# A drain at the end of each of TensorE's steps, and two buffers moved out of their pools, in a graph network layer

## The chip, the core and the metric

The kernel runs on one core of a Trainium2 chip. The core has TensorE (PE in the profile; its weight loads are PEld), VectorE (DVE), ScalarE (ACT), GpSimd (POOL) and SyncE (SP). Each works through its own queue in order, and they wait for one another by semaphores. The metric is the time of one execution on the device in microseconds (us). Of the kernel before there are 17 runs.

## The reference

One layer of message passing on a graph, with a residual and a layer norm. There are 12,500 nodes of 64 features and 212,500 edges of 32 features, sorted by their destination. All is float32.

```python
msg_in = concatenate([nodes[row], nodes[col], edge_features])        # 64 + 64 + 32
messages = relu(msg_in @ mW1 + mb1) @ mW2 + mb2                      # 128, then 64
aggregated = segment_sum(messages, col, num_segments=nodes.shape[0])
upd_in = concatenate([nodes, aggregated])
x = layernorm(nodes + relu(upd_in @ uW1 + ub1) @ uW2 + ub2)
```

Here `row` is an edge's source and `col` its destination.

## The kernel before, in words

Edges are worked in 554 groups (`G`) of 384 (`GE`), each three tiles of 128. Since edges are sorted, the destinations of one group lie in a window of 32 nodes (`W`) from a start that DVE reads into a register. The second product of the message MLP is folded into the update, so that only the hidden layer (128 wide) is summed for each node.

A group `g` goes through three parts on TensorE, each in a bank of its own of one of two PSUM buffers (`own.ps[g % 2]`):

- `turn` (L360): three transposes of the gathered source rows and of the one-hot of destinations beside them. ACT copies the result into `own.st` (L372), where edge features already lie, and keeps the counts.
- `hidden` (L392): three products with `wm`, which holds the source's weights, the window's 32 rows (the destinations' share of the first layer) and the edge features' weights. ACT applies the relu (L401).
- `sums` (L419, L422): one small transpose of the counts and three products that add the hidden rows to the window's nodes. DVE adds them to `agg` (L431) and the counts to a row of `xc` (L432).

A *step* `k` (`step`, L502) puts these parts together on TensorE's queue: turn of group `k`, hidden of `k - 2`, sums of `k - 4`. Once in four steps, for a block of four groups (`SB`), one more product follows at the step's end: `windows` (L310), the columns of destinations `xw` with `w1b`. DVE copies its four parts into the `wm` tiles (L315). All waits of a step are laid on its first instruction, and all but its last instruction raise no semaphore. What follows a step waits for that last instruction, `did[-1]`: ACT's copy and relu, DVE's adds and copies, and the load of edge features for a later block (SP, L284). In the last ten groups (`SHORT`) the parts are steps of their own.

Gathers run on POOL's queue, one indirect DMA for each tile of 128 rows (L145), 16 groups ahead (`AHEAD`) in a ring of 20 (`RING`). The gather of group `g` waits for ACT's copy of group `g - 20`. In 52 groups the middle tile is not gathered: DVE (L349) or ACT (L350) copies its 128 columns one by one from `xc`, the transposed nodes on the chip, a few after each step (`copies_of`). These are the copied columns.

DVE's queue has, in the order of the program: the one-hot of group `k + 1` (L324), the adds of step `k`, with the window step the four `wm` copies, the column copies, and once in four steps the copies of destinations' columns into `xw` (L303). TensorE's step `k + 2` uses the same PSUM buffer as step `k`, and so waits for ACT's copy and relu and for DVE's adds of step `k`.

Twenty-five times, when a run of 512 nodes has all of its edges, `update` puts its own products into TensorE's queue behind a step (L449, L450, in the next step L462). They write a PSUM buffer from a pool, and ACT (L452) and DVE (L464) wait for them by TensorE's semaphore.

`own` holds buffers allocated outside the pools, for which the framework tracks nothing: their order is what `after` says (L109). Before the change, `xw` is a pool of two tiles and `w1b` a tile of the pool of constants; the product L310, which reads both, is then always the last of its step.

Of the kernel before, what the change touches and what calls it, by code (L numbers as in the profile page):

```python
# [10 lines left out]
F32 = mybir.dt.float32  # L11
# [11 lines left out]
D = 64  # L23
DE = 32
H = 128
# [3 lines left out]
W = 32  # L29
TG = 3  # L30
GE = TG * P
G = (E + GE - 1) // GE
SB = 4
# [3 lines left out]
NW = 2 * SB  # L37
# [3 lines left out]
CH = 512  # L41
# [3 lines left out]
SHORT = 10  # L45
# [36 lines left out]
class Own:  # L82
# [4 lines left out]
    def __init__(self, nc, ctx):  # L87
        def on(name, *shape, of=nc.sbuf_tensor):
            return ctx.enter_context(of(name, list(shape), F32)).ap()

        self.s = [on(f"own_s{i}", P, TG, D + W) for i in range(RING)]
        self.st = [on(f"own_st{i}", P, SB * GE) for i in range(BLOCKS)]
        self.wm = [on(f"own_wm{i}", P, H) for i in range(NW)]
        self.h = [on(f"own_h{i}", P, TG, H) for i in range(NH)]

        self.f = {way: [on(f"own_f{len(way)}_{i}", P, P) for i in range(2)]
                  for way in (BY_DVE, BY_ACT)}
        self.ident = on("own_ident", P, P)
        self.counts = on("own_counts", D + W, G)

        self.ps = [on(f"own_ps{i}", P, 3, 512, of=nc.psum_tensor) for i in range(2)]
# [3 lines left out]
def ordered(ctx: ExitStack, tc: tile.TileContext, a, own, ok):  # L105
# [3 lines left out]
    nc = tc.nc  # L109
    x, out = a["x"], a["out"]  # L110
    const = ctx.enter_context(tc.tile_pool(name="const", bufs=1))
    xwp = ctx.enter_context(tc.tile_pool(name="xw", bufs=2))
    iop = ctx.enter_context(tc.tile_pool(name="iota_ps", bufs=1, space=PSUM))
    ups = ctx.enter_context(tc.tile_pool(name="upd_ps", bufs=1, space=PSUM))
    early = ctx.enter_context(ExitStack())
# [9 lines left out]
    nc.sync.dma_start(src_sb[:, :first], a["src"][:, :first])  # L125

    loads, places_by, copy_by, relu_by, sums_by, wm_by, turn_by = ({} for _ in range(7))
    efs_by, hidden_by, columns_by = {}, {}, {}
    held = {ET.DVE: [], ET.Activation: []}

    def after(first, *others):

        tc.declare_no_dep(first.ins, group="quiet", reason="waits for the last of a step")
        for i in others:
            tc.add_manual_dep(
                first.ins, i.ins.name,
                mybir.DependencyInfo(mybir.DependencyClass.Sync, mybir.DependencyReason.DATA),
                reason="the kernel's own rings",
            )
        return first  # L140
# [36 lines left out]
    xc = const.tile([D + 2, NP], F32, name="xc")  # L177
# [4 lines left out]
    nc.sync.dma_start(dlc_i, a["dst_cols"])  # L182
    nc.sync.dma_start(xc[D : D + 1, :].rearrange("o (p n) -> o p n", p=P), zero)
    nc.sync.dma_start(xc[D + 1 :, :].rearrange("o (p n) -> o p n", p=P), ones[:, : NP // P])
    w1b = const.tile([D + 2, H], F32, name="w1b")
    nc.vector.memset(w1b[D : D + 1, :], 0.0)
    nc.scalar.dma_start(w1b[:D, :], a["mW1"][D : 2 * D, :])
    nc.scalar.dma_start(w1b[D + 1 :, :], a["mb1"][None, :])
# [102 lines left out]
    def places(b):  # L291

        g, n = b * SB, min(SB, G - b * SB)
        if n <= 0:
            return
        _, v = nc.values_load_multi_w_load_instructions(
            start_i[0:1, g : g + n], engines=[ET.DVE], min_val=0, max_val=N - 1,
            skip_runtime_bounds_check_because="they were clamped to the nodes on the chip",
        )
        xw = xwp.tile([D + 2, SB, W], F32, name="xw")  # L300
        for i in range(n):
            starts[g + i] = v[i]
            nc.vector.tensor_copy(xw[:, i, :], xc[:, bass.ds(v[i], W)])  # L303
        xws[b] = xw, n

    def windows(b, wp, own_bank=True):


        xw, n = xws.pop(b)
        did = nc.tensor.matmul(wp[: n * W, :], xw[:, :n, :], w1b, start=True, stop=True)  # L310

        def copies():
            for i in range(n):
                g = b * SB + i
                c = nc.vector.tensor_copy(wm[g % NW][D : D + W, :], wp[i * W : (i + 1) * W, :])  # L315
                after(c, *([did] if own_bank else []), *([hidden_by[g - NW]] if g >= NW else []))
                wm_by[g] = c

        return did, copies

    def onehot(g):
        if g >= G:
            return
        places_by[g] = nc.vector.tensor_tensor(  # L324
            own.s[g % RING][:, :, D:], iota.unsqueeze(1).to_broadcast([P, TG, W]),
            dlc[:, g * TG : (g + 1) * TG].unsqueeze(2).to_broadcast([P, TG, W]), ALU.is_equal,
        )
        after(places_by[g], *([sums_by[g - RING]] if g >= RING else []))
# [161 lines left out]
    def step_update(g):  # L490

        nonlocal now
        if not now and waiting and waiting[0][0] <= g:
            steps = waiting.pop(0)[1]
            now = [steps[0](), *steps[1:]]
        elif now:
            got = now[1](now[0])
            now = [got, *now[2:]] if len(now) > 2 else []
# [3 lines left out]
    def step(*work):  # L502


        parts, used = [], []
        for part, g in work:
            ps, old = own.ps[g % 2], users[part][g % 2]
            parts.append((part, g, *part(g, ps)))
            used += old
        did = [i for p in parts for i in p[2]]  # L510
        after(did[0], *used, *(i for p in parts for i in p[3]))
        copies = None
        for part, g, *_ in parts:
            if part is sums:
                for b in [b for b in xws if (b - 1) * SB <= g][:1]:
                    last, copies = windows(b, own.ps[g % 2][:, 2, (TIMES + 1) * W :][:, :H])
                    did.append(last)
        for i in did[:-1]:
            tc.no_tile_sem_insts.add(i.ins.name)
            tc.add_to_no_dep_group("quiet", i.ins)  # L520
        for part, g, _, _, follow in parts:
            if part is sums:
                step_update(g)
            users[part][g % 2] = follow(did[-1])
            if part is sums and copies:
                copies()
                users[part][g % 2] += [wm_by[b * SB + i] for i in range(min(SB, G - b * SB))]

    inputs(0)
    inputs(1)  # L530
    places(0)
    windows(0, ups.tile([H, CH], F32, name="u_ps")[:, :H], False)[1]()
    onehot(0)
    made = summed = 0

    for k in range(G):
        if k < BITS:
            bit(k)
        if k % SB == 2:
            inputs(k // SB + 2)  # L540
        if k % SB == 1:
            places(k // SB + 1)
        onehot(k + 1)
        if k < G - SHORT:
            step((turn, k), *([(hidden, k - 2)] if k > 1 else []),
                 *([(sums, k - 4)] if k > 3 else []))
            made, summed = max(0, k - 1), max(0, k - 3)
        else:

            step((turn, k))  # L550
            for _ in range(2):
                if summed < made:
                    step((sums, summed))
                    summed += 1
            for _ in range(2):
                if made <= k:
                    step((hidden, made))
                    made += 1
        if k + AHEAD < G:
            gather(k + AHEAD)  # L560
        copies_of(k)
# [285 lines left out]
@with_exitstack  # L847
def gnn_layer(ctx: ExitStack, nc, a):
    own = Own(nc, ctx)
    tc = ctx.enter_context(tile.TileContext(nc))  # L850
    flag = ctx.enter_context(tc.tile_pool(name="flag", bufs=1))
    ok = flag.tile([1, 1], I32, name="ok")
    with tc.manual_schedule():
        ordered(tc, a, own, ok)
    good = nc.values_load(ok[0:1, 0:1], min_val=0, max_val=1,
                          skip_runtime_bounds_check_because="a comparison's result")
    with tc.If(good == 0):
        with tc.manual_schedule():
            unordered(tc, a)
# [36 lines left out]
```

## Time and profile before

| | us |
|---|---|
| median of 17 runs | 2686.57 |
| lowest, highest | 2680.12, 2695.09 |
| the profiled execution | 2690.23 |
| its span, first to last instruction | 2688.4 |

| engine | busy us | share of the span |
|---|---|---|
| TensorE, products | 1677.7 | 62% |
| TensorE, weight loads | 1448.7 | 54% |
| GpSimd (gathers) | 1519.0 | 57% |
| VectorE | 1060.7 | 39% |
| ScalarE | 827.1 | 31% |

The mean granted clock of TensorE is 0.79 of full speed. A group of the profile has its line, engine, operation and tiles (what it writes, then what it reads), the count, busy time and mean duration, and then the engine's idle time just before these instructions, with what ended most of it. "Issue" as a releaser is time in which the profile shows nothing waited for; "remote" is a releaser that it couldn't name. A product in float32 is recorded as two products and two weight loads. Ends of products are modelled.

### The profile page before, as it was taken

How to read it: one execution, taken by the hardware profiler on the slowest of the kernel's cores; microseconds unless marked ns; L12 is line 12 of the kernel's file. 1: busy time of each engine (PE TensorE's matmuls, PEld its weight loads, DVE VectorE, ACT ScalarE, POOL GpSimd, SP SyncE). 2: the span in 40 equal slices, each digit the busy share in tenths (PEclk: the TensorE clock that was granted, in tenths of full speed). 3: DMA queues.
4: the chain of work that ended last, by engine and by line, in shares of the span. 5: the costliest groups of instructions: out<-in, count | busy, mean ns of one | idle time of the engine just before them, and what ended most of it. 6: DMA issues, size and time to landing. Idle time of an engine off the chain costs nothing.

```text
span 2688.4 us, 45023 instructions
## 1 busy us (share of the span) xinstructions
PE 1677.7 (62%) x9545; PEld 1448.7 (54%) x9545; DVE 1060.7 (39%) x7163; ACT 827.1 (31%) x4455; POOL 1519.0 (57%) x1616
## 2 busy tenths in 40 slices
PE   0466666666666765665656665757566666666577
PEld 0355555555555655555645555656555555555565
DVE  4124344344343443443434434444344343443423
ACT  0123333333333333333323333333333333332322
POOL 7565555555555555555555555555555555555550
PEclk9677777778777777878778778788777777887878
DMA  3211111111111111111111111111111111111110
GB/s 76 62 40 37 35 32 36 33 34 34 33 37 32 35 35 34 32 36 33 34 32 34 37 29 37 32 35 34 35 32 36 30 36 31 35 37 32 35 33 14
DMA packets 71877, 95.29 MB, mean 35 GB/s; under 512 B 32632, under 2 KB 40075, under 8 KB 71595
## 3 DMA queue, kind: packets, MB, share of 16 engines
q0 software_dynamic: 51488, 52.80, 10.3%
q1 hardware_dynamic: 19193, 39.06, 5.3%
q8 instruction: 81, 1.33, 0.2%
q14 instruction: 201, 1.65, 0.2%
q10 hardware_dynamic: 914, 0.46, 0.1%
HBM read 88.90 MB, written 3.20 MB: 34 GB/s over the span
## 4 chain that ended last, share of the span: by engine, by line
PE 48%; issue 18%; another core or an unknown queue 18%; ACT 10%; ACTq 3%; DVE 3%; DMA 0%; DVEq 0%
PE own_ps L422 18%; PE own_ps L392 15%; PE own_ps L360 9%; ACT own_h L401 3%; ACT own_st L372 3%; ACT own_f L350 3%; ACTq L343 2%; PE own_ps L419 2%; PE u_ps L462 1%; PE u_ps L449 1%; ACTq L350 1%; PE own_ps L310 1%; PE u_ps L450 1%; DVE agg L431 1%
## 5 line engine op out<-in xcount | busy, mean ns | idle before, releaser
L145 POOL DMA_INDIRECT own_s<-in_x,src_sb x1609 | 1518.2, 944 | 1091.4 <-ACT own_st L372 670.4
L360 PE MATMUL own_ps<-own_ident,own_s 128*96 128x128 f32 x1661 | 364.9, 342 | 915.7 <-issue 736.9
L372 ACT ACTIVATE own_st<-own_ps 96x384 f32<-96x384 f32 (+2 forms) x606 | 286.2, 472 | 1703.3 <-PE own_ps L422 1043.6
L360 PEld LDWEIGHTS own_ps<-own_ident,own_s 128*96 128x96 f32 x1661 | 225.6, 159 | 992.6 <-issue 794.2
L422 PE MATMUL own_ps<-own_s,own_h 128*128 128x128 f32 x3322 | 641.6, 341 | 0.1
L392 PE MATMUL own_ps<-own_wm,own_st 128*128 128x128 f32 (+1 forms) x3322 | 628.2, 337 | 1.4 <-DVE own_wm L315 1.4
L431 DVE TENSOR_TENSOR agg<-own_ps,agg 128x32 f32 x554 | 105.3, 190 | 1218.0 <-ACT own_h L401 1119.0
L392 PEld LDWEIGHTS own_ps<-own_wm,own_st 128*128 128x128 f32 (+1 forms) x3322 | 569.5, 250 | 16.3 <-issue 11.3
L422 PEld LDWEIGHTS own_ps<-own_s,own_h 128*128 128x128 f32 x3322 | 520.1, 234 | 27.1
L349 DVE COPY own_f<-xc 64x1 f32 x3968 | 428.4, 144 | 213.9 <-issue 209.1
L350 ACT ACTIVATE own_f<-xc 64x1 f32 x2688 | 304.4, 193 | 8.7 <-issue 5.9
L401 ACT ACTIVATE own_h<-own_ps 128x384 f32<-128x384 f32 x553 | 263.3, 476 | 18.8 <-PE own_ps L392 13.5
L315 DVE COPY own_wm<-own_ps 32x128 f32<-32x128 f32 x550 | 157.0, 285 | 5.9 <-issue 0.3
L324 DVE TENSOR_TENSOR own_s<-iota,dlc 128x96 f32<-128x96 f32 x554 | 135.9, 246 | 12.3 <-issue 7.1
L432 DVE TENSOR_TENSOR xc<-own_ps,xc 1x32 f32 x554 | 101.1, 183 | 27.8 <-PE u_ps L450 5.9
L419 PE MATMUL own_ps<-own_ident,own_counts 32*1 32x32 f32 x554 | 106.9, 193 | 3.8 <-ACT own_st L372 1.9
L372 ACT ACTIVATION_READ_ACCUMULATOR own_st<-own_ps 96x1 f32 (+1 forms) x554 | 106.4, 192 | 0.6
L303 DVE COPY xw<-xc 66x32 f32 x554 | 80.0, 210 | 50.2 <-issue 49.3
L419 PEld LDWEIGHTS own_ps<-own_ident,own_counts 32*1 32x1 f32 x554 | 41.1, 74 | 93.7 <-issue 47.5
L310 PE MATMUL own_ps<-w1b,xw 66*128 66x128 f32 (+1 forms) x276 | 57.1, 290 | 0.0
L462 PE MATMUL u_ps<-u,u 128*128 128x64 f32 (+1 forms) x196 | 48.7, 398 | 9.8 <-ACT u L452 9.8
L462 PEld LDWEIGHTS u_ps<-u,u 128*128 128x128 f32 (+1 forms) x196 | 47.2, 324 | 11.3 <-ACT u L452 11.1
(63 smaller groups left out, 337.1 us busy)
## 6 DMA issues: line engine op xcount, KB each, us to landing
own_st<-in_efT SPq DMA_DIRECT2D x138, 192.0 KB
own_s<-in_x,src_sb POOLq DMA_INDIRECT x1609
xin<-in_x SPq DMA_DIRECT2D x24, 128.0 KB
out<-o SPq DMA_DIRECT2D x24, 128.0 KB
xc<-in_xT SPq DMA_DIRECT2D x12, 179.2 KB
dlc_i<-in_dst_cols SPq DMA_DIRECT2D x1, 831.0 KB
xc<-in_xT SPq DMA_DIRECT2D x4, 179.5 KB
src_sb<-in_src SPq DMA_DIRECT2D x13, 50.5 KB
```

The source lines that it names most:

```text
L145: nc.gpsimd.indirect_dma_start(out=s[:p, j, :D], out_offset=None, in_=x[:, :], in_offset=bass.IndirectOffsetOnAxis(ap=src_sb[:p, g * TG + ...
L315: c = nc.vector.tensor_copy(wm[g % NW][D : D + W, :], wp[i * W : (i + 1) * W, :])
L324: places_by[g] = nc.vector.tensor_tensor(own.s[g % RING][:, :, D:], iota.unsqueeze(1).to_broadcast([P, TG, W]), dlc[:, g * TG : (g + 1) * ...
L349: c = (nc.vector.tensor_copy(*column) if engine == ET.DVE else nc.scalar.activation(*column, AF.Copy))
L350: else nc.scalar.activation(*column, AF.Copy))
L360: nc.tensor.transpose(xt[:, j * P : j * P + p], s[:p, j, :], ident[:p, :p])
L372: nc.scalar.activation(t[to, c : c + m], xt[to, :m], AF.Copy, **({"accum_out": counts[to, g : g + 1]} if to.stop > D else {})), step)
L392: did.append(nc.tensor.matmul(pre[:p, j, :], edges, weights, start=i == 0, stop=i == len(parts) - 1))
L401: relu_by[g] = [nc.scalar.activation(h, pre, AF.Relu)]
L419: did = [nc.tensor.transpose(line, counts[lo:, g : g + 1], ident[lo : D + W, lo : D + W])]
L422: did.append(nc.tensor.matmul(sg, h[:p, j, :], s[:p, j, D:].unsqueeze(1).to_broadcast([p, TIMES, W]), start=j == 0, stop=j == len(sizes) - 1))
L431: after(nc.vector.tensor_tensor(agg[:, at], sg[:, 0, :], agg[:, at], ALU.add), step),
```

## The change

At the end of each step, behind its last product and ahead of any update's products, TensorE gets a `drain`: an instruction of its sequencer that waits until the engine has finished. It comes in every step whose first part has a group under 544 (`G - SHORT`). The drain becomes `did[-1]`; so all products of a step, the window product too, raise no semaphore, and what followed the last product now waits for the drain. That drain's semaphore belongs to TensorE's sequencer, another one than the engine's own. The products of the updates keep the engine's own.

So that L310 can be one of the silent instructions, its operands `xw` (two buffers) and `w1b` are moved to `own`. The order that the pool kept is written out: DVE's copies into `xw` for block `b` wait for the step that read the buffer for block `b - 2` (`wide_by`).

```diff
@@ class Own
+        self.xw = [on(f"own_xw{i}", D + 2, SB, W) for i in range(2)]
+        self.w1b = on("own_w1b", D + 2, H)
@@ ordered
-    xwp = ctx.enter_context(tc.tile_pool(name="xw", bufs=2))
...
-    w1b = const.tile([D + 2, H], F32, name="w1b")
+    w1b = own.w1b
@@ places
-        xw = xwp.tile([D + 2, SB, W], F32, name="xw")
+        xw = own.xw[b % 2]
         for i in range(n):
             starts[g + i] = v[i]
-            nc.vector.tensor_copy(xw[:, i, :], xc[:, bass.ds(v[i], W)])
+            after(nc.vector.tensor_copy(xw[:, i, :], xc[:, bass.ds(v[i], W)]),
+                  *([wide_by[b - 2]] if b > 1 else []))
@@ windows
-        def copies():
+        def copies(step):
+            wide_by[b] = step
             for i in range(n):
                 g = b * SB + i
                 c = nc.vector.tensor_copy(wm[g % NW][D : D + W, :], wp[i * W : (i + 1) * W, :])
-                after(c, *([did] if own_bank else []), *([hidden_by[g - NW]] if g >= NW else []))
+                after(c, step, *([hidden_by[g - NW]] if g >= NW else []))
@@ step
+        if work[0][1] < G - SHORT:
+            did.append(nc.tensor.drain())
         for i in did[:-1]:
             tc.no_tile_sem_insts.add(i.ins.name)
...
             if part is sums and copies:
-                copies()
+                copies(did[-1])
@@ before the loop
-    windows(0, ups.tile([H, CH], F32, name="u_ps")[:, :H], False)[1]()
+    did, copies = windows(0, ups.tile([H, CH], F32, name="u_ps")[:, :H])
+    copies(did)
```

More of the change, by code (lines that the diff above doesn't have):

```diff
@@ L127, in ordered @@
     loads, places_by, copy_by, relu_by, sums_by, wm_by, turn_by = ({} for _ in range(7))
-    efs_by, hidden_by, columns_by = {}, {}, {}
+    efs_by, hidden_by, columns_by, wide_by = {}, {}, {}, {}
     held = {ET.DVE: [], ET.Activation: []}
@@ L299, in places, with windows @@
         )
-        xw = xwp.tile([D + 2, SB, W], F32, name="xw")
+        xw = own.xw[b % 2]
         for i in range(n):
             starts[g + i] = v[i]
-            nc.vector.tensor_copy(xw[:, i, :], xc[:, bass.ds(v[i], W)])
+            after(nc.vector.tensor_copy(xw[:, i, :], xc[:, bass.ds(v[i], W)]),
+                  *([wide_by[b - 2]] if b > 1 else []))
         xws[b] = xw, n
-    def windows(b, wp, own_bank=True):
+    def windows(b, wp):
         xw, n = xws.pop(b)
         did = nc.tensor.matmul(wp[: n * W, :], xw[:, :n, :], w1b, start=True, stop=True)
-        def copies():
+        def copies(step):
+            wide_by[b] = step
             for i in range(n):
```

## The prediction, made before the changed kernel ran

> **What bounds the kernel now.** I read the page's totals first, then the waits, then the timeline of a few steps, then the end of the kernel. No engine is full, and GpSimd (POOL) with its gathers is the one with most left to do one after the other:
>
> ```profile
> PE 1677.7 (62%) x9545; PEld 1448.7 (54%) x9545; DVE 1060.7 (39%) x7163; ACT 827.1 (31%) x4455; POOL 1519.0 (57%) x1616
> ...
> PEclk9677777778777777878778778788777777887878
> ...
> L145 POOL DMA_INDIRECT own_s<-in_x,src_sb x1609 | 1518.2, 944 | 1091.4 <-ACT own_st L372 670.4
> ```
>
> The waits say who holds whom; the columns are engine and line, what released it, us in total, times, longest:
>
> ```profile
> DVE agg L431 <- ACT own_h L401: 1119.0, 289, 45.6
> ACT own_st L372 <- PE own_ps L422: 1043.6, 248, 6.9
> PEld own_ps L360 <- issue: 794.2, 273, 10.2
> ...
> POOL own_s L145 <- ACT own_st L372: 670.4, 271, 9.9
> ACT own_st L372 <- remote: 494.0, 80, 18.7
> ```
>
> POOL waits 670 us for ScalarE's copy of a step (the ring of gathered tiles is full), DVE waits for ACT, ACT waits for TensorE, and TensorE waits in turn. A circle of waits has a slow link somewhere. The timeline shows it (start, duration, engine, line; idle time before in brackets):
>
> ```profile
> 1480.13 0.39 PE L310 MATMUL own_ps<-w1b,xw 66*128 66x128 f32 x2
> ...
> 1481.92 0.94 PE L422 MATMUL own_ps<-own_s,own_h 128*128 128x128 f32 x6
> 1482.04 0.94 POOL L145 DMA_INDIRECT own_s<-in_x,src_sb  x1 [0.30 <-issue]
> 1484.55 0.49 ACT L372 ACTIVATE own_st<-own_ps 96x384 f32<-96x384 f32 x1 [5.62 <-remote]
> ...
> 1485.39 0.94 POOL L145 DMA_INDIRECT own_s<-in_x,src_sb  x1 [2.41 <-ACT own_st L372]
> ...
> 1489.27 0.85 PE L360 MATMUL own_ps<-own_ident,own_s 128*96 128x128 f32 x3 [6.42 <-issue]
> ```
>
> The step that ends with L310 is over at 1480.52, and ACT, idle, starts its copy only at 1484.55. TensorE has meanwhile done the whole next step (to 1482.86). So the array is not late; the semaphore that its last matmul raises is. Pairing every step with its copy over steps 20 to 530, 125 of the 127 paired steps that end with L310 are copied over 0.5 us late, median 3.96 us; of 383 that end with L422, 190 are (in part behind a late one), 165 within 0.06 us. A late release comes 1.49 us (median) after the last gather of an unbroken run of gathers, about when its DMAs have landed. One turn of the circle is then: 0.55 us from release to the next gather, six gathers at 1.249 us (two steps' worth), 1.49 us to the next release, together 9.53 us for two steps. Four steps in the trace take 19.04 us (median from L310 step to L310 step), so this is what sets the time. After the last gather it stops:
>
> ```profile
> 2623.70 0.94 PE L422 MATMUL own_ps<-own_s,own_h 128*128 128x128 f32 x6
> ...
> 2628.45 0.39 PE L310 MATMUL own_ps<-w1b,xw 66*128 66x128 f32 x2
> ```
> ```profile
> 2624.67 0.49 ACT L372 ACTIVATE own_st<-own_ps 96x384 f32<-96x384 f32 x1 [2.37 <-PE own_ps L422]
> ...
> 2628.87 0.49 ACT L372 ACTIVATE own_st<-own_ps 96x384 f32<-96x384 f32 x1 [1.26 <-PE own_ps L310]
> ```
>
> The L422 of 2623.70 ends at 2624.64 and the copy starts at 2624.67; the same L310 is answered in 0.03 us (2628.84 to 2628.87). So L310 itself is not slow; its semaphore is held while gathers run.
>
> **The change part by part.** *Added: 550 drains* (544 turning steps, four sums and two hidden steps of the tail), one behind each step's last matmul on TensorE's queue. Only the drain still raises a semaphore, through the sequencer. ACT's copy, its relu, DVE's adds and wm copies, SP's edge-feature load and a few early gathers now wait for it. Queued behind the drain are the update's matmuls (L449, L450, L462) and the next step: its two or three semaphore waits, first weight load and first matmul. The cost of one drain: the trace's own drain on this queue takes 8 ns, but it has not stood behind matmuls here, so the price is bounded. Below: nothing, where TensorE waits for data anyway. Above, where steps run on end: semaphore 0.014 us after the modelled end, three waits about 0.106 us apart, 0.07 us to the weight load, 0.03 us to the matmul, 0.44 us, and the 0.16 to 0.21 us by which steps overlap now is lost: 0.6 us, 550 times 330 us. I take the lower end plus nothing, because TensorE's cover is there: a step takes 2.16 us at full clock, 2.8 with the drain, and POOL needs 1609 x 1.249 / 554 = 3.63 us a step. If that cover goes (half clock, 3.84 us a step), it is a rival below.
>
> *Moved: the step's signal.* No row shows a drain with a semaphore while gathers run. Ends: released at the array's end as after 2613 us (0.03 us), or held as now (3.96 us). I take the first: the array had finished the next step during the hold, EVENT_SEMAPHORE instructions of TensorE's sequencer ran on during it, and DVE's and ACT's own semaphores arrive about 0.01 us after their instructions' ends in the middle of runs of gathers. It is a choice between two mechanisms, not a measured price. [...] No run here yet shows a drain held.
>
> *Destinations' columns and w1b outside pools.* The same copies (L303 x554, 0.21 us) and load; DVE's copies wait for the drain of two blocks earlier, over 15 us old. Nothing, and if that wait did come last it would be on DVE, ahead of the next one-hot, which the next step but one needs.
>
> *What is late next: POOL.* First gather at 2.96 us; 1609 x 1.249 = 2009.5. The circle's stops are gone except where something still holds: in the windows from 50 to 150 us there are 64 gathers, 79.9 us of 100, so 20 us of early idle stay. After the last gather there are 77 us now, with TensorE 20 groups behind; with TensorE close behind POOL it is nearer the last stretch (2640 to 2688, 48 us): 60 taken. The updates' matmuls keep TensorE's own semaphore. With POOL running without a break these stay held until the ring fills, and each hold costs POOL one release and restart, 1.49 + 0.55: 25 updates x 2 x 2.04 = 102 us. Sum: 2.96 + 2009.5 + 20 + 60 + 102 = 2194 of span; the profiled execution has 1.8 us beside its span (2690.23 against 2688.4) and lies 3.7 us over the median of 2686.57, so 2192. Bounds: no hold at the updates and a 48 us tail, no early idle, 2060; drains at 0.25 us on top of everything, 2330. DVE stays under POOL: adds, one-hot, eight column copies with their register load, and a quarter of a block's wm and xw copies come to about 2.9 us a step.
>
> **The rivals.**
> *Signal prompt, TensorE the bound at half clock.* The clock events against TensorE's busy share in each 3.41 us window: of 143 windows at half clock under 0.9 busy none was followed by full clock, of 188 above most were; at full clock all 132 under 0.45 fell, of 271 over 0.55 four. Drain gaps of 0.45 us in 4.29 leave many windows below 0.9. Held there: 554 x 4.29 = 2377, first turn at 57, tail 48, updates' matmuls 112: 2594. Against: windows that miss most of a gap still raise it, and at full clock 2.16 of 3.63 us is 0.6.
>
> *The drain does not do what it says, and nothing moves.* The circle stays 9.53 us per two steps: 2690. It needs the held step to cost nothing more, which the next one speaks against.
>
> *The other side: the drain is held as the matmul was.* Place: TensorE's queue behind the drain of the L310 step. The step now done during the hold starts after it, so a release frees one copy instead of two, and POOL's run is three gathers: 0.55 + 3.75 + 1.49 = 5.79 us for one step in place of 4.76. On all steps that is +570, on half of them +285: 2975 at half, down to 2690 where every second drain passes between two runs; I say 2950. Against steps that pass at POOL's 3.63 us, it decides from the share f of held steps where 5.79 f + 3.63 (1 - f) is 4.76, 52%. For it: completions seem to come in order (late ones of two steps arrive 0.16 us apart).
>
> **How the numbers follow.** Prompt signal, POOL bound: 0.46, 2060 to 2330, 2192. Prompt signal, clock bound: 0.14, 2330 to 2620. Within 0.2% (5.4 us, about what the runs can tell): 0.04. Drain held: 0.36, 2700 to 3260, half of it under 2960. Faster 0.60, slower 0.36. The range takes the first two, the third and the lower half of the last: 2060 to 2960.
>
> **What would show it.** Right: the copy L372 starts within 0.1 us of the drain in the middle of a run of gathers; POOL's wait for ACT falls from 670 to about 100 us and its gathers stand 1.25 us apart nearly throughout; POOL near 70% busy. Wrong: drains of some us with gathers running, and TensorE's first L360 waiting behind them; or POOL still waiting and PEclk near 5. I'd be wrong also if gathers, run without a break, slow each other.

## The result: 3.2% slower, and the profile after

The changed kernel takes 2773.93 us (median), the kernel before 2688.01: a ratio of 1.0322, with a 95% interval of 1.0307 to 1.0338. The forecast of 2192 had the wrong sign. The profiled execution has a span of 2766.6 us against 2688.4, 78.2 more.

The page of the kernel after, its totals, the clock and the gathers' group:

```profile
PE 1878.8 (68%) x9545; PEld 1576.1 (57%) x9545; DVE 1070.3 (39%) x7163; ACT 845.7 (31%) x4455; POOL 1523.4 (55%) x1616
...
PEclk9888777676776767778767866767767767676778
...
L147 POOL DMA_INDIRECT own_s<-in_x,src_sb x1609 | 1522.6, 946 | 1163.3 <-ACT own_st L376 713.2
```

TensorE's same 9545 matmuls take 201 us more busy time, because the granted clock fell from 0.790 to 0.742: of the 3322 products of the sums (L422, now L426) 1661 run at half clock in place of 965, and one takes 0.42 us there against 0.28 at full clock. POOL's own work is unchanged (1522.6 us against 1518.2), but it stands idle for 72 us more. The gathers tell where the span went: the first starts at 2.96 us in both kernels, the last ends at 2687.5 in place of 2611.2, and what follows takes 79.2 us in place of 77.3. So 76 of the 78 us were lost while gathers ran.

The waits of the kernel after:

```profile
ACT own_st L376 <- PEq L523: 1460.2, 431, 17.9
DVE agg L435 <- ACT own_h L405: 1033.2, 351, 45.6
PEld own_ps L364 <- issue: 793.6, 477, 17.0
POOL own_s L147 <- ACT own_st L376: 713.2, 322, 9.9
```

The circle of waits is still there. It has one new member: ACT now waits for the drain (L523, on TensorE's sequencer, PEq). POOL's wait for ACT, which was to fall from 670 to 100 us, rose to 713.

The timeline of a few steps after:

```profile
1495.35 1.65 PE L426 MATMUL own_ps<-own_s,own_h 128*128 128x128 f32 x6
1497.44 0.49 ACT L376 ACTIVATE own_st<-own_ps 96x384 f32<-96x384 f32 x1 [6.25 <-PEq L523]
1497.67 0.84 PE L364 MATMUL own_ps<-own_ident,own_s 128*96 128x128 f32 x3 [0.67 <-issue]
...
1498.29 0.95 POOL L147 DMA_INDIRECT own_s<-in_x,src_sb  x1 [2.45 <-ACT own_st L376]
...
1499.86 1.65 PE L426 MATMUL own_ps<-own_s,own_h 128*128 128x128 f32 x6
...
1501.62 0.49 ACT L376 ACTIVATE own_st<-own_ps 96x384 f32<-96x384 f32 x1 [2.67 <-PEq L523]
1501.88 0.84 PE L364 MATMUL own_ps<-own_ident,own_s 128*96 128x128 f32 x3 [0.38 <-issue]
...
1504.97 0.94 POOL L147 DMA_INDIRECT own_s<-in_x,src_sb  x1 [0.30 <-issue]
...
1505.51 0.63 PE L313 MATMUL own_ps<-own_w1b,own_xw 66*128 66x128 f32 x2
1507.15 0.49 ACT L376 ACTIVATE own_st<-own_ps 96x384 f32<-96x384 f32 x1 [3.88 <-PEq L523]
1507.38 0.51 PE L364 MATMUL own_ps<-own_ident,own_s 128*96 128x128 f32 x3 [1.23 <-issue]
...
1508.00 0.94 POOL L147 DMA_INDIRECT own_s<-in_x,src_sb  x1 [2.09 <-ACT own_st L376]
```

Read three steps here. The one that ends at 1497.00 (1495.35 + 1.65) is answered 0.44 us later. The one that ends at 1501.51 is answered at 1501.62, 0.11 us later, although gathers run: it ended 3.2 us after POOL's run of gathers began. The one that ends at 1506.14 (1505.51 + 0.63) is answered 1.01 us later, and that is 1.24 us after the last gather of the run has ended (1505.91). So the drain is held, as the matmul was. In all three TensorE's next L364 starts only after ACT's copy has begun. In the kernel before, the array did a whole step in such a hold (a hold is the time by which a signal comes late).

Two counts over the same steps put numbers on both. Of the copies that ACT stood ready for, 176 of 359 came over 0.5 us late before (median 3.64 us) and 195 of 497 after (median 2.40). And of 510 steps, 257 were followed by a step that began before their own copy did; after the change 3 were.

The trace has a record of every drain, and it shows the hold directly. For the 195 late copies the drain itself ends 2.30 us (median) after the array's modelled end, for the other 302 it ends 0.02 us after, and none of the 550 drains ends sooner than that. In both groups ACT's copy starts 0.10 us after the drain's end. Behind a late drain, TensorE's next step begins 0.32 us (median) after the drain's end.

### The profile page after: what moved, and what is told of

Same layout as the page of the kernel before. It is cut to its first block, busy times and chain, and to the rows that moved or that the text cites. A ratio compares the mean times of both kernels' runs of the same rounds, so it can differ in the third digit from the quotient of the medians.

```text
span 2766.6 us, 45620 instructions
## 1 busy us (share of the span) xinstructions
PE 1878.8 (68%) x9545; PEld 1576.1 (57%) x9545; DVE 1070.3 (39%) x7163; ACT 845.7 (31%) x4455; POOL 1523.4 (55%) x1616
## 3 DMA queue, kind: packets, MB, share of 16 engines
q14 instruction: 201, 1.65, 0.2%
## 4 chain that ended last, share of the span: by engine, by line
issue 29%; PEld 27%; PEldq 14%; PE 11%; POOL 9%; DVE 6%; ACT 2%; DVEq 1%; ACTq 1%; DMA 0%; POOLq 0%
PEld own_ps L396 12%; PEldq L523 12%; PEld own_ps L426 11%; POOL own_s L147 9%; PE own_ps L426 3%; PEld own_ps L364 3%; PE own_ps L396 2%; PEldq L364 2%; PE u_ps L466 2%; PE own_ps L364 1%; DVE own_f L353 1%; PE u_ps L453 1%; DVE own_wm L319 1%; PE u_ps L454 1%; ACT own_h L405 1%
## 5 line engine op out<-in xcount | busy, mean ns | idle before, releaser
L147 POOL DMA_INDIRECT own_s<-in_x,src_sb x1609 | 1522.6, 946 | 1163.3 <-ACT own_st L376 713.2
L364 PE MATMUL own_ps<-own_ident,own_s 128*96 128x128 f32 x1661 | 376.6, 350 | 782.3 <-issue 585.0
L426 PE MATMUL own_ps<-own_s,own_h 128*128 128x128 f32 x3322 | 728.3, 375 | 0.0
L364 PEld LDWEIGHTS own_ps<-own_ident,own_s 128*96 128x96 f32 x1661 | 207.6, 158 | 912.9 <-issue 793.6
L396 PE MATMUL own_ps<-own_wm,own_st 128*128 128x128 f32 (+1 forms) x3322 | 677.3, 357 | 1.6 <-DVE own_wm L319 1.3
L396 PEld LDWEIGHTS own_ps<-own_wm,own_st 128*128 128x128 f32 (+1 forms) x3322 | 615.4, 269 | 15.2 <-issue 7.6
L426 PEld LDWEIGHTS own_ps<-own_s,own_h 128*128 128x128 f32 x3322 | 596.1, 264 | 29.0
L354 ACT ACTIVATE own_f<-xc 64x1 f32 x2688 | 305.3, 192 | 11.5 <-issue 6.4
L436 DVE TENSOR_TENSOR xc<-own_ps,xc 1x32 f32 x554 | 101.1, 183 | 43.0 <-PE u_ps L454 21.5
L305 DVE COPY own_xw<-xc 66x32 f32 x554 | 77.3, 205 | 47.6 <-issue 46.7
L313 PE MATMUL own_ps<-own_w1b,own_xw 66*128 66x128 f32 (+1 forms) x276 | 61.6, 310 | 0.0
```

The costliest lines, as they stand in the source:

```text
L147: nc.gpsimd.indirect_dma_start(out=s[:p, j, :D], out_offset=None, in_=x[:, :], in_offset=bass.IndirectOffsetOnAxis(ap=src_sb[:p, g * TG + ...
L354: else nc.scalar.activation(*column, AF.Copy))
L364: nc.tensor.transpose(xt[:, j * P : j * P + p], s[:p, j, :], ident[:p, :p])
L396: did.append(nc.tensor.matmul(pre[:p, j, :], edges, weights, start=i == 0, stop=i == len(parts) - 1))
L426: did.append(nc.tensor.matmul(sg, h[:p, j, :], s[:p, j, D:].unsqueeze(1).to_broadcast([p, TIMES, W]), start=j == 0, stop=j == len(sizes) - 1))
```

## The experiments

Theory A is the third rival: the drain is held while gathers run, as the matmul was, and the next step, which used to run during the hold, waits behind it. Theory B is that a drain has a price on TensorE whether it is held or not: the array empties, and the gap lets the clock fall.

**The chips differ.** The runs fell on several chips, and they are of two kinds, which I had not expected. On three of them the kernel before takes 2659 to 2662 us, and in the traces of the experiments run there copies are late as in the first profile. On the three others it takes 2037 us, and in the traces taken there not one copy that ACT stood ready for is over 0.5 us late. (Of the kernel before itself there is one trace, from where it takes 2688 us.) I call them chips that hold and chips that do not. Ratios below are always to the kernel before on the same chip, and each price has to be found on both kinds.

**1. The parts, where nothing is held.** The buffers moved without drains, then drains in three arrangements:

```
k1_moved_only            -        if work[0][1] < G - SHORT:
                         -            did.append(nc.tensor.drain())
k2_drain_unsignalled     the drain behind the step, the last matmul keeps the semaphore:
                         +            d = nc.tensor.drain()
                         +            tc.no_tile_sem_insts.add(d.ins.name)
k3_window_steps          +        if work[0][1] < G - SHORT and copies:
k4_other_steps           +        if work[0][1] < G - SHORT and not copies:
```

> The destinations' columns and w1b outside pools, no drains: the last matmul of a step raises the semaphore, as before. Theory A (the drain is held while gathers run, as the matmul was, and keeps the next step from running during the hold) and theory B (a drain costs TensorE 0.1 to 0.6 us whoever waits, and its gaps lower the clock) both expect the time of before, 2680 to 2697 us, four steps in 19.05 us, POOL in runs of six gathers. Theory C (the buffers' move costs) expects 2730 to 2774.

> A drain behind each step's last matmul, but the matmul keeps the semaphore; nobody waits for the drain but TensorE's own queue. Theory A: a held drain keeps the next step back whoever signals, 2755 to 2790 us, runs of three gathers as after. Theory B: 2740 to 2790 as well, with the clock at 0.74. If what costs is that the sequencer's semaphore reaches ScalarE later than the matmul's, 2680 to 2700.

> Drains only in the 138 steps that end with the window product (a quarter). Theory A: these are the steps that were held in the kernel before (125 of 127), so most of the loss stays: 2740 to 2790 us. Theory B: a quarter of the price, 2700 to 2720.

> Drains only in the steps without a window product (three quarters, 412). Theory A: about half of these steps are late and the window step's own hold still lets the next step run: 2690 to 2740 us. Theory B: three quarters of the price, 2740 to 2770.

Measured: k1 0.9998 (0.9989 to 1.0007), k2 1.0266 (1.0251 to 1.0282), k3 0.9997 (0.9988 to 1.0006), k4 1.0304 (1.0246 to 1.0362). The buffers' move costs nothing, and theory C falls. The absolute times of the expectations mean nothing here, because this chip does not hold; but it shows a price that theory A does not have: drains cost 2.7 to 3.0% with no semaphore held. The price is not the same for each drain: the 138 of k3 cost nothing, and the 412 of k4 no less than the 550 of k2. In k4 the drains also carry the signal, which there comes 0.117 us after the array's end and in k2 0.037; how much of k4's price that is was not tested apart.

Where it comes from is seen in k1's page and waits,

```profile
PE 1473.5 (72%) x9545; PEld 1261.4 (62%) x9545; DVE 1057.4 (52%) x7163; ACT 843.2 (41%) x4455; POOL 1520.8 (75%) x1616
...
PE own_ps L364 <- DVE agg L435: 135.6, 67, 3.4
```

beside those of k2:

```profile
PE 1572.6 (75%) x9545; PEld 1320.9 (63%) x9545; DVE 1058.3 (51%) x7163; ACT 843.1 (40%) x4455; POOL 1521.4 (73%) x1616
...
PE own_ps L364 <- DVE agg L435: 220.4, 102, 3.1
```

TensorE is busy 99 us longer (clock 0.906 to 0.863) and idle 52 us less (562.8 to 510.4), together the 47 us by which the span grew. The shortest gaps between steps were an overlap of 0.21 us and are now a stand of 0.32. POOL is hardly touched: its last gather ends at 2017.1 in place of 2013.0 us. But 66 us are left behind it in place of 23: at the last gather TensorE has 15 groups still to turn, in k1 4.

**2. The changed kernel again, and the clock.** To ask whether the clock is the price, k6 gives TensorE more work, so that a window of 3.41 us at half clock is fuller: in the trace before, none of 143 such windows under 0.9 busy was followed by full clock, of 188 above 150 were (`TIMES` says how often the sums' products write the same 32 columns side by side; DVE reads the first):

```
k5_after            the changed kernel
k6_after_wide_sums  -TIMES = 4
                    +TIMES = 8
```

> The changed kernel itself, beside the kernel before on the same chip. In the last runs the kernel before took 2036.7 us in place of 2688: no copy was late (481 of 481 within 0.06 us), POOL's gathers ran without a break, and drains in three quarters of the steps cost 3.0%, with the matmul keeping the semaphore 2.7% for all steps. Theory B (a drain's gap and the clock it lets fall): 2090 to 2130 us where no semaphore is held, 1.027 to 1.045 of before; every copy 0.117 us after the array. Theory A (the held drain is what costs): 1.00 to 1.01 of before wherever before has no held semaphore; and 1.03 where before takes 2688.

> The changed kernel with the sums' matmuls twice as wide (256 columns in place of 128, the same sums once more): more work for TensorE, 3 x 0.157 us a step at full clock, 0.31 at half. At half clock a step then fills about 0.91 of its time with the drain's gap, in place of 0.895, and a window over 0.9 is what raises the clock. If the clock is what the drains cost, the time stays or falls (2040 to 2110 us where no semaphore is held), with a granted clock over 0.90; if the gap itself or TensorE's sum of work is what costs, it rises by up to 0.3 us a step: 2130 to 2280.

This chip holds: k5 1.0308 (1.0287 to 1.0329). The 3 x 0.157 us a step was my estimate; no run shows a product of 256 columns by itself. In the trace before, a product of 512 columns takes 0.59 us at full clock (L449, L450) and one of 128 columns 0.28 (L422). In k6 the granted clock rose from 0.745 to 0.882, higher than in any kernel on a chip that holds, and the time rose as well, from 2740.9 to 2778.6 us, 1.0472 (1.0410 to 1.0534) of before. A higher clock did not bring the time back. By itself this does not clear the clock, because the wider sums also keep TensorE busy 92 us longer (1960.8 against 1868.6). But two kernels below do: k17 takes 3.9% less than the kernel before at a lower clock (0.741 in its trace, the kernel before 0.779 to 0.792 on that chip), and k18 at 0.683 takes no longer than the changed kernel there at 0.732. So in these runs, where semaphores are held, the granted clock does not set the time.

**3. The parts, where semaphores are held, and more steps in flight.** Three kernels of the first group again, and one without drains but with three sets of PSUM banks in place of two, so that a step waits for the copies of the step three before it:

```
k7_three_sets   -[on(f"own_ps{i}", P, 3, 512, ...) for i in range(2)]
                +[on(f"own_ps{i}", P, 2, 512, ...) for i in range(SETS)]
                -TIMES = 4
                +TIMES = 3
                +SETS = 3
                -[(hidden, k - 2)] if k > 1 else []     -[(sums, k - 4)] if k > 3 else []
                +[(hidden, k - 3)] if k > 2 else []     +[(sums, k - 6)] if k > 5 else []
                (and % 2 becomes % SETS; sums and windows move into the two banks)
```

> No drains. Three sets of PSUM banks in place of two, so that a step waits for the copies of the step three before it, not two (the hidden part is three groups behind the turn, the sums six; the sums are repeated three times, not four, to fit). Where semaphores are held while gathers run, theory A says that a release then frees three copies: runs of nine gathers, 0.55 + 9 x 1.249 + 1.49 = 13.28 us for three steps, 4.43 a step in place of 4.76, about 0.93 to 0.96 of the kernel before. If the hold is a fixed delay of a step's signal and not bound to the gathers' end, 0.98 to 1.02. Where no semaphore is held, POOL's gathers set the time and nothing is gained: 0.995 to 1.005.

> A drain behind each step's last matmul, which keeps the semaphore: nobody but TensorE's own queue waits for the drain. It took 1.027 of before on a chip whose semaphores were not held. On one that holds them, theory A: a held drain keeps the next step back whoever signals: 1.025 to 1.045, and POOL's runs are of three gathers. Theory D (it is the signal through the sequencer that comes late, not the standing still): 1.00 to 1.01.

> Drains only in the 138 steps that end with the window product. Where no semaphore is held it took 1.000 of before. On a chip that holds them, theory A: those are the steps held longest (3.96 us), behind each of them the next step now waits: 1.01 to 1.03. Theory B (the gap and the clock alone): 1.00, as where nothing is held.

> Drains only in the other 412 steps; it took 1.030 where no semaphore is held. On a chip that holds them, theory A: the step behind a held window step still runs during the hold, so runs of six gathers stay: 1.00 to 1.015. Theory B: 1.02 to 1.03 as where nothing is held.

Measured, on a chip that holds: k7 0.9933 (0.9911 to 0.9954), k8 1.0244 (1.0198 to 1.0289), k9 1.0013 (0.9992 to 1.0033), k10 1.0144 (1.0117 to 1.0172).

k8 speaks for theory A and against D: a drain that signals nobody costs most of the loss, in none of 510 steps did the next one begin before the copy, and 184 copies were still over 0.5 us late, with the matmul's own semaphore. The drain's record shows the same hold: for these 184 it ends 2.00 us (median) after the array's modelled end, within 0.01 us of the copy's start, and for the others 0.05 us; the next step begins 0.28 us after a late drain's end. The signal's change of place from matmul to sequencer does not make it prompt, and its absence does not save the time.

k10 lies at the upper end of what theory A expected. k9 is a miss of theory A: drains in the steps that had been held longest cost nothing. Its timeline shows what I had left out. Around 1495 us of its trace the window step is the second of the two steps done in one hold: it ends at 1495.64 us, its predecessor at 1492.80, and both are copied from 1495.57 on. There nothing is behind the drain that could have run. The steps had changed places against POOL's runs. Of the 128 window steps among the 510, 25 began before the copy of the step ahead of them in the kernel before, and 66 do so in k9; so this holds for about half of them. Next steps that begin ahead of the copy fell from 257 to 185, and for the other half of the drains it is not shown why they cost nothing.

k7 is a second miss: three sets, and POOL still runs in sixes. Its timeline shows why:

```profile
1488.86 0.49 ACT L377 ACTIVATE own_st<-own_ps 96x384 f32<-96x384 f32 x1 [6.63 <-PE own_ps L427]
...
1489.84 0.19 DVE L436 TENSOR_TENSOR agg<-own_ps,agg 128x32 f32 x1 [4.92 <-ACT own_h L406]
...
1490.82 0.96 DVE L354 COPY own_f<-xc 64x1 f32 x8 [0.57 <-issue]
...
1491.70 0.24 DVE L329 TENSOR_TENSOR own_s<-iota,dlc 128x96 f32<-128x96 f32 x1
...
1492.04 0.42 PE L365 MATMUL own_ps<-own_ident,own_s 128*96 128x128 f32 x1 [0.52 <-issue]
```

The one-hot that the step of 1492.04 needs (L329) is ready at 1491.94. It stands on DVE's queue behind an add (L436) that waited 4.92 us for the held signal. DVE did its queue in order here (L436 at 1489.84, L354 at 1490.82, L329 at 1491.70), and so kept the number of steps in flight at two.

**4. The one-hot one step earlier, without and with drains.**

```
k11, k14, k17   k7, and  -        onehot(k + 1)
                         +        onehot(k + 2)
k12, k15, k18   the same, with the drain as the step's last instruction
```

> Three sets of PSUM banks without drains gained only 0.7% where semaphores are held, and POOL still ran in sixes. Its trace says why: DVE works in order, and its one-hot for step k+1 stands behind its adds of step k-1, which wait for that step's held signal; so only two steps could be in flight. Here the one-hot is made one step earlier. Theory A on a chip that holds: three steps per release, runs of nine gathers, 4.43 us a step in place of about 4.68, 0.92 to 0.97 of the kernel before. If it is not the number of steps in flight that sets the run of gathers: 0.985 to 1.00. Where nothing is held: 0.995 to 1.005.

> The same three sets and early one-hot, with a drain at the end of every step that carries the signal. Theory A on a chip that holds: behind a held drain no step runs however many sets there are, so the gain of the three sets is gone: 1.00 to 1.03, runs of three gathers (the changed kernel took 1.031 and 1.032). If the drains' cost is a price by the drain (0.1 to 0.17 us each), it keeps the three sets' gain and adds some 3%: 0.95 to 1.00. Where nothing is held: 1.025 to 1.045, as with drains in two sets.

That pair fell on a chip that does not hold, and so did its repeat:

> Three sets of banks and the earlier one-hot, no drains; it took 1.001 of before on a chip where no semaphore is held. On a chip that holds, theory A: up to three steps per release, runs of nine gathers, 0.92 to 0.97 of before. If it is not the number of steps in flight that sets POOL's runs: 0.985 to 1.00.

> The same with drains that carry the signal; it took 1.003 of before where nothing is held, so three sets hide a drain's price there. On a chip that holds, theory A: no step runs behind a held drain however many sets there are: 1.00 to 1.03, runs of three gathers. If the drains' cost is the price that three sets hide: as without drains, within 0.01 of the other run.

Without drains 1.0014 (1.0004 to 1.0023) and 1.0008 (0.9998 to 1.0017), with drains 1.0028 (1.0013 to 1.0043) and 1.0039 (1.0025 to 1.0053). So with three steps in flight the drains' 2.7 to 3.0% shrinks to 0.1 to 0.3% where nothing is held: the price is there, but TensorE has room for it. Part of the room may be the sums' fourth repeat, which these kernels leave out.

The third pair fell on a chip that holds, together with the changed kernel:

> The changed kernel itself. Where semaphores are held it took 1.031 and 1.032 of before. Where none is held it has not run: with two sets of banks, drains behind all steps without the signal took 1.027, drains with the signal in three quarters of the steps 1.030; so 1.03 to 1.045, TensorE's granted clock near 0.85, every copy 0.117 us after the array.

> Three sets and the earlier one-hot, no drains; 1.001 of before on two chips where no semaphore is held. On a chip that holds, theory A: three steps per release, runs of nine gathers, 0.92 to 0.97 of before. If it is not the number of steps in flight that sets POOL's runs: 0.985 to 1.00.

> The same with drains that carry the signal; 1.003 and 1.004 of before where nothing is held. On a chip that holds, theory A: no step runs behind a held drain however many sets there are: 1.00 to 1.03, runs of three gathers. If the drains' cost is a price per drain that three sets hide: within 0.01 of the run without drains.

Measured: k16 1.0287 (1.0256 to 1.0318), k17 0.9611 (0.9588 to 0.9633), k18 1.0266 (1.0218 to 1.0314). This separates the theories: three sets gain 3.9% without drains, and with drains all of it is gone, 6.8% between two kernels that differ in the drains alone (2734.38 against 2560.15 us). A price that three sets hide would have left k18 at k17. The timeline of k17, without drains:

```profile
1521.84 0.49 PE L365 MATMUL own_ps<-own_ident,own_s 128*96 128x128 f32 x3
...
1523.80 0.49 PE L365 MATMUL own_ps<-own_ident,own_s 128*96 128x128 f32 x3
...
1525.94 0.49 ACT L377 ACTIVATE own_st<-own_ps 96x384 f32<-96x384 f32 x1 [6.23 <-remote]
...
1526.79 0.95 POOL L148 DMA_INDIRECT own_s<-in_x,src_sb  x1 [2.24 <-ACT own_st L377]
1527.35 0.47 ACT L377 ACTIVATE own_st<-own_ps 96x384 f32<-96x384 f32 x1
...
1528.65 0.48 ACT L377 ACTIVATE own_st<-own_ps 96x384 f32<-96x384 f32 x1
```

Two more steps begin (1521.84, 1523.80) while the first is held; at the release three copies follow one another, and POOL's next run is nine gathers. The waits of k18, with drains:

```profile
ACT own_st L377 <- PEq L524: 1325.9, 405, 24.1
DVE agg L436 <- ACT own_h L406: 1006.7, 358, 41.6
PEld own_ps L365 <- issue: 744.6, 517, 18.9
POOL own_s L148 <- ACT own_st L377: 664.8, 331, 10.1
```

They look like those of the changed kernel, as if the third set were not there. The counts side by side, each from one trace of a chip that holds (a stop is a pause of over 0.6 us between two gathers):

| kernel | POOL's stops | mean us | commonest run | next step begins before the copy |
|---|---|---|---|---|
| before | 281 | 2.44 | 6 gathers (188 of 282) | 257 of 510 |
| after | 397 | 1.98 | 3 (217 of 398) | 3 |
| k17, three sets | 205 | 2.59 | 9 (90 of 206) | 425 |
| k18, three sets and drains | 421 | 1.77 | 3 (276 of 422) | 16 |

Between before and after the stops add up to 684 and 786 us, 101 more; the 116 fewer places where one gather follows another at once give back 29, and the gathers themselves take 4 more. That is the 76 us by which the last gather is later.

**5. Without gathers.** SP loads rows with plain DMAs in the gathers' place, so other rows than the reference's:

```
k13_rows_by_sp   -nc.gpsimd.indirect_dma_start(out=s[:p, j, :D], ..., in_=x[:, :], ...)
                 +nc.sync.dma_start(s[:p, j, :D], x[g * 20 + j : g * 20 + j + p, :])
```

> No drains and no gathers: the rows are loaded by SP's plain DMAs (128 rows of 256 bytes each, one after the other in memory, so other rows than the reference's), as many and into the same places; POOL is idle. On a chip that holds semaphores: if POOL's gathers hold them, no copy is late and TensorE sets the time, 1400 to 1800 us; if it is the landing of DMAs as such, copies are late by some us again, and 2000 us or more. Where nothing is held it shows TensorE's own time, 1400 to 1800 us.

It fell on a chip that does not hold, so whether POOL's gathers are what holds the semaphores stays open. But it missed what I expected of the time: 2013.45 us, not 1400 to 1800. With POOL idle (0.8 us busy) the chain that ended last is

```profile
PE 69%; issue 13%; ACT 10%; DVE 4%; ACTq 3%; SPq 1%; DMA 1%; DVEq 0%
```

From step 20 to step 530 TensorE with its waits for ACT and DVE takes 3.53 us a step by itself, in this one run. In k1, where POOL's gathers run without a stop, a step takes 3.62 us, and in k2, with the drains, 3.73. So in this kernel TensorE and POOL are nearly level: by these three numbers a drain adds an estimated 0.20 us to TensorE's turn (3.73 - 3.53), and only 0.09 of it (3.62 - 3.53) is covered. What is left fits the drains' price where nothing is held, 0.10 us each (53 us for 550 in k2).

## Why the prediction was wrong

**The step that failed** is "Moved: the step's signal". I chose between two mechanisms and took the drain's signal as prompt, 0.03 us, because the sequencer's own instructions ran on during a hold (EVENT_SEMAPHORE at 1480.77 and 1480.88 in the trace before, in the hold from 1480.52 to 1484.55). In the trace after, 195 of 497 copies came over 0.5 us behind the array, and late ones were released 1.47 us (median) after the last gather of a run, as before (1.51). Behind the late copies the drains' own records end 2.30 us (after) and 2.00 us (k8) past the array's modelled end, and in k8 no step began behind a drain before the copy of the step ahead.

**The drains at no cost** was the second wrong step. The cover that I named was POOL's 3.63 us a step against TensorE's 2.16 with 0.6. A step's own work is not its turn: with the waits for ACT and DVE TensorE's turn is 3.53 us (k13), so a step had 0.09 us of cover against POOL's 3.62 of k1, in place of the 1.47 that I counted (3.63 - 2.16). Where nothing is held 550 drains cost 53 us (2089.91 against 2036.66), 0.10 us each, inside my bounds of 0 to 330 us but not at the end that I took. With a third set of banks there is cover, and 0.1 to 0.3% is left.

**The rival that came true** had the right mechanism and place, "a release frees one copy instead of two, and POOL's run is three gathers", and a stop of 0.55 + 1.49 = 2.04 us on top of the 0.30 that lie before every gather, 2.35 in all, where 1.98 was measured. Its size, 2950 us, was too large, and its rule that it decides from 52% of held steps was wrong: 39% were late, and it decided. I priced the other steps at POOL's 3.63 us. In fact, of the steps that end in the first four microseconds of a run of gathers, 198 of 268 are answered within 0.5 us, and of those that end later in it none of 93. So 127 of 398 runs are still of six gathers, but POOL stops 397 times in place of 281, and the mean step (steps 20 to 530) came to 4.88 us against 4.74.

**The half-clock rival** saw the clock fall, and it did, to 0.742; k17 and k18 show that where semaphores are held this is not what sets the time. **Nothing moves** is excluded by the interval. **The buffers outside the pools** cost nothing, as said: 0.9998.

**The circle** of 9.53 us for two steps was right in its sum, though not in one term: the timeline has 0.84 us from the release to the next gather (1484.55 to 1485.39), not 0.55, and the sum comes out because six gathers at 1.249 us already hold the 0.30 us before the first. Made one step longer it predicted 13.28 us for three, 4.43 a step, and k17 took 4.50. **The POOL-bound sum** of 2194 us can be held against the chips that do not hold. Its first term is right (k1's gathers take 2010.0 us from the first start to the last end, 2009.5 said), the 20 us of early idle were part of the hold and are gone, and the tail is 23 us, not 60. The 102 us for held updates have no counterpart there, since POOL does not stop once in k1. The changed kernel itself was not run there.

## What to carry to other kernels

Count the steps that are in flight while a signal is late. In these runs an instruction that makes an engine wait for its own end took this overlap away even where nobody waited for it (k8, 1.0244 of before: no next step began ahead of the copy, against 257 of 510 before), and its price was then not its own duration but the work that used to run behind it. Before a late signal is chased, see what else can be done during the delay: here a third set of banks and a one-hot made one step earlier (with the sums' fourth repeat left out) gave 3.9% (2560.15 us against 2661.88), and changed the time by 0.1% where no signal is late; and every engine's queue in the circle must allow the extra step, not the banks alone (k7, with three sets and the one-hot where it was, took 0.9933 of before, k17 0.9611).

## What the runs showed of the hardware

The same program takes 2037 us on some chips and 2659 to 2688 on others. With the time goes the hold: on the first no copy is over 0.5 us late (0 of 482 that ACT stood ready for, in k1), in the kernel before 176 of 359 are. With it goes another difference: for the 1609 gathers the trace of k1 (no hold) has 25563 landing events, 15.9 a gather, that of the kernel before 7400 (4.6), that of the changed kernel 8636 (5.4). What holds the signals, and whether the fewer events and the hold have one cause, is open. Every run on record comes with a span from its trace, so none shows the time without tracing.

Where nothing is held, a drain that signals is answered 0.117 us after the array's modelled end (k12), a matmul 0.037 (k1).
